# A window-attention start reordered: x alone on the queues, the fold around the group norm, tokens in 16 loads, norms spread two at a time

## The chip, the core and the metric

The kernel runs on one core of a Trainium2 chip. Its time is the device time of one execution in microseconds (us); lower is better. The core has a matrix engine (PE), a vector engine (DVE), an activation engine (ACT), GpSimd (POOL) and a synchronising engine (SP) that issues transfers. Each runs its own stream of instructions in order; they meet at semaphores. SP, ACT and POOL can issue DMA transfers, and all transfers share 16 DMA engines. PE writes to PSUM, from which the others copy ("evacuate") to SBUF.

## What is computed

The input is an image of 256 channels and 64 x 64 positions. Cut to what matters here:

```python
# layer 0: window attention over a group-normed image
xn = group_norm(x)                                # 32 groups of 8 channels
q, k = sigmoid(Wq xn), sigmoid(Wk xn)             # 8 heads of 32 channels
v = Wv xn, each head's vector scaled to length 1
for w in (1, 2, 4):                               # box of 64, 32, 16 positions a side
    attn = q . box_sum(k v^T)
    norm = q . box_sum(k)
    outs.append(attn / (norm + 1e-6))
x = x + Wout concat(outs) + bout
# layer 1: tokens of 256 values, causal attention with Wq, bq, Wk, bk, Wv, bv,
# a small feed-forward, then a mixture of two of eight experts
```

The causal layer's scores need only products of its weights, Wq^T Wk and its bias terms. The kernel works those out once, at its start ("the fold"), and parks them in DRAM until the causal layer.

## The kernel before, in words

`window_attention` loads the image `x` (4 MB) in four chunks of 1024 positions; each chunk comes in two transfers, channel half 0 on SP's queue and half 1 on ACT's. Then it issues, in the program's order, the six mask tables on ACT, the fold, the 32 token loads on SP (`t`, the image again with positions as rows) and `bo`, the output bias, on POOL. The group norm follows: `bn_stats` on DVE over half 0 and then half 1, a matmul with `groups` that averages over 8 channels (L264), four small DVE steps, a second such matmul (L272), a square root on ACT and a reciprocal on DVE. `norm` holds the means and scales with which DVE writes normalised chunks (L612).

`folded` (L743 to L800) transposes both weights on PE (L763), copies them with DVE (L764), multiplies them (L775, once per half `c`), forms the bias terms by matmuls of one column (L780, L785, L792), and writes four results to DRAM on SP (L798). It has a pool of its own.

`window_heads` runs twice, for head groups `hg` 0 and 1 (128 channels each). It projects each chunk to k and q (L519) and to v (L542), turns k (L575) and sums blocks (L586). What stands in the list `late` is run at chunk 0, behind its values. Then come two loops over "lists", each of which fills a 512-column PSUM bank for each of four heads. The first loop has 45 lists along columns of the image, the second 93 along eight strips `Y` of eight rows. `push` handles a list: mask matmuls (L353), score matmuls (L362, four heads on four groups of 32 rows), evacuation (L330 on ACT for five of eight, L332 on DVE), and, for the list before, the sums with v (L395, in `add`). PSUM has six rotating buffers for this, and two for the sums.

`norms` gives the steps for one strip's norms: `sum_up`, four `invert` steps, and three `spread_out` steps, each of which spreads one window's norm over the heads by a matmul (L479) and copies it (L482, ACT). `inner` (four or three DVE steps) prepares the inner part that `inside` feeds to PE (L414), `convolve` is the output projection (L507), `boxes` makes POOL work for the next strip. In the second loop `plan(at, tasks)` puts one task behind each list from number `at` on; `firsts[Y]` is a strip's first list.

PE and POOL follow the program's order in these loops, and in the list loops DVE and ACT too (`manual_schedule`). Elsewhere a scheduler orders each engine's work by when it expects it to be ready.

Of the kernel before, what the change touches and what calls it, by code (L numbers as in the profile page):

```python
# [19 lines left out]
P = 128  # L20
# [132 lines left out]
@with_exitstack  # L153
def conv_attn_hybrid(ctx: ExitStack, tc: tile.TileContext, a, out):
    nc = tc.nc

    const = ctx.enter_context(tc.tile_pool(name="const", bufs=1))
    ident = const.tile([P, P], F32, name="ident")
    make_identity(nc, ident)
    eps5 = const.tile([P, 1], F32, name="eps5")  # L160
    nc.vector.memset(eps5, 1e-5)

    tok = ctx.enter_context(tc.tile_pool(name="tok", bufs=1))
    t = tok.tile([P, NT, D], F32, name="t")

    dram = ctx.enter_context(tc.tile_pool(name="folded", bufs=1, space=bass.MemoryType.DRAM))
    low = ctx.enter_context(tc.tile_pool(name="low", bufs=1))
    iks = ctx.enter_context(tc.tile_pool(name="iks", bufs=1, reuse_waits="tile"))
    causal = Causal(tc, a, t, ident, eps5, low, iks)
    window_attention(tc, a, t, eps5, ident, causal, lambda psum: folded(tc, dram, psum, a, ident))  # L170
    big = ctx.enter_context(tc.tile_pool(name="l12big", bufs=1, reuse_waits="tile"))
    keep = ctx.enter_context(tc.tile_pool(name="l12keep", bufs=1, reuse_waits="tile"))
    given = Given(nc, a, keep, causal)
    x2 = causal_attention(tc, t, ident, eps5, causal, big, given)
    experts(tc, a, t, out, ident, eps5, given, x2)


def window_attention(tc, a, t, eps5, ident, causal, first):
# [5 lines left out]
    with ExitStack() as ctx:  # L184
# [23 lines left out]
        raws.append(load(3, vh.rearrange("p j e -> p (j e)")[:, 0:2048].rearrange("p (c n) -> p c n", c=DC)))  # L208
        tables = []
# [5 lines left out]
        causal.fold = first(psum)  # L215
        for i in range(NT):
            nc.sync.dma_start(out=t[:, i, :], in_=a["xT"][i * P : (i + 1) * P, :])
        bo = w.tile([P, D], F32, name="l0bo")
        nc.gpsimd.dma_start(out=bo, in_=a["L0_bout"].partition_broadcast(P))
# [30 lines left out]
        pt = psum()  # L250
        wide = sm.tile([P, 4, 32], F32, name="wide", bufs=1)
        nc.vector.tensor_copy(wide, sums.unsqueeze(1).to_broadcast([P, 4, 32]))
        nc.tensor.transpose(pt[:, 0:P], wide.rearrange("p w j -> p (w j)"), ident)
        nc.vector.tensor_copy(spreadh, pt[:, 0:P])


        mv = sm.tile([P, DC, 2], F32, name="mv")
        for c in range(DC):
            st = sm.tile([P, NQ, 6], F32, name="st")
            for j in range(NQ):  # L260
                nc.vector.bn_stats(out=st[:, j, :], in_=raws[j // 2][:, c, (j % 2) * 512 : (j % 2 + 1) * 512])
            nc.vector.bn_aggr(out=mv[:, c, :], in_=st)
        pm = psum()
        nc.tensor.matmul(pm[:, 0:DC], lhsT=groups, rhs=mv[:, :, 0], start=True, stop=True)  # L264
        gm = w.tile([P, DC], F32, name="gm")
        nc.vector.tensor_copy(gm, pm[:, 0:DC])
        d2 = sm.tile([P, DC], F32, name="d2")
        nc.vector.tensor_sub(d2, mv[:, :, 0], gm)
        nc.vector.tensor_mul(d2, d2, d2)
        nc.vector.tensor_add(d2, d2, mv[:, :, 1])  # L270
        pv = psum()
        nc.tensor.matmul(pv[:, 0:DC], lhsT=groups, rhs=d2, start=True, stop=True)  # L272
        rs = w.tile([P, DC], F32, name="rs")
        nc.scalar.activation(rs, pv[:, 0:DC], AF.Sqrt, bias=eps5)
        nc.vector.reciprocal(rs, rs)
        norm = [(gm[:, c : c + 1], rs[:, c : c + 1]) for c in range(DC)]

        late = []
# [19 lines left out]
def window_heads(tc, a, t, ident, hg, norm, raws, load, psum, pools, tables, consts, late, causal):  # L298
# [13 lines left out]
    nc.gpsimd.dma_start(out=wo, in_=a["L0_Wout"].rearrange("(w g p) e -> g p w e", g=2, p=P)[hg])  # L312
# [149 lines left out]
    def norms(boxed, rns):  # L462
# [14 lines left out]
        def spread_out(wi):  # L477
            pn = psum()
            nc.tensor.matmul(pn, lhsT=spreadh[32 * wi : 32 * wi + 32, :], rhs=r[32 * wi : 32 * wi + 32, :],  # L479
                             start=True, stop=True)  # L480
            rn = state["h"].tile([P, 512], F32, name=f"rn{wi}")
            nc.scalar.copy(rn, pn)  # L482
            rns.append(rn)

        return [sum_up] + [lambda j=j: invert(j) for j in range(4)], [lambda wi=wi: spread_out(wi) for wi in range(3)]
# [106 lines left out]
    with tc.manual_schedule(engines={mybir.EngineType.PE, mybir.EngineType.Pool}), ExitStack() as keys:  # L592
        with ExitStack() as vctx:
# [25 lines left out]
            for m in range(4):  # L619
                if m < 3:  # L620
                    normalise(m + 1)
                project(gs[m], m)
                values(gs[m], m)
                if m == 0:
                    while late:
                        late.pop(0)()
                if m:
                    block_sums(kp, m - 1)
                kp = turned(m)
# [14 lines left out]
            for m in range(4):  # L644
                for s in range(2):
                    for b in range(2):
# [4 lines left out]
                        )  # L651
            if hg == 0:
# [3 lines left out]

            steps, spreads = norms(boxed, strips[0]["rn"])
            for i, parts in enumerate(lists[1:]):
                push(parts)
                if i >= len(lists) - 9 and steps:  # L660
                    steps.pop(0)()
# [24 lines left out]
        for Y in range(8):  # L686
            at, after = firsts[Y], firsts[Y + 1]
            plan(at, lambda Y=Y: (outer(1, Y), outer(2, Y)))
            plan(at + 1, *(lambda wi=wi, Y=Y: strips[Y]["st"].append(inner(wi, Y)) for wi in (1, 2)))
            if Y == 0:  # L690
                plan(at + 1, *spreads)
            if Y < 7:
                plan(at, lambda Y=Y: ahead(Y + 1))
                end = plan(max(after - 5, at + 6), *(lambda n=n, Y=Y: got[Y + 1][0][n]() for n in range(5)))
                plan(max(end, after + 1), *(lambda n=n, Y=Y: got[Y + 1][1][n]() for n in range(3)))
# [47 lines left out]
def folded(tc, dram, psum, a, ident):  # L743
# [3 lines left out]
    with ExitStack() as tmp:  # L747
        s = tmp.enter_context(tc.tile_pool(name="foldsm", bufs=1, side="right"))
        mm = s.tile([P, DC, D], F32, name="mm")
        mb = s.tile([P, DC], F32, name="mb")  # L750
        wvu = s.tile([P, DC, D + 2], F32, name="wvu")
        nc.gpsimd.memset(wvu[:, :, 0:1], 0.0)
        bvc = s.tile([P, D + 2], F32, name="bvc")
        nc.gpsimd.memset(bvc[:, 0:1], 1.0)
        wT = {}
        for name in ("Wq", "Wk"):
            src = s.tile([P, DC, D], F32, name=f"f{name}")
            nc.scalar.dma_start(out=src, in_=a["L1_" + name].rearrange("(c p) e -> p c e", p=P))
            dst = s.tile([P, DC, D], F32, name=f"t{name}")
            for e in range(DC):  # L760
                pt = psum()[:, 0:D]
                for c in range(DC):
                    nc.tensor.transpose(pt[:, c * P : (c + 1) * P], src[:, c, e * P : (e + 1) * P], ident)  # L763
                nc.vector.tensor_copy(dst[:, e, :], pt)  # L764
            wT[name] = dst
        col = {}
        for name in ("bq", "bk"):
            col[name] = s.tile([P, DC], F32, name=f"f{name}")
            nc.scalar.dma_start(out=col[name], in_=a["L1_" + name].rearrange("(c p) -> p c", p=P))
        nc.scalar.dma_start(out=wvu[:, :, 1 : D + 1], in_=a["L1_Wv"].rearrange("(c p) e -> p c e", p=P))  # L770
        nc.scalar.dma_start(out=bvc[:, 1 : D + 1], in_=a["L1_bv"].partition_broadcast(P))
        for c in range(DC):
            pm = psum()[:, 0:D]
            for e in range(DC):
                nc.tensor.matmul(pm, lhsT=wT["Wq"][:, e, c * P : (c + 1) * P], rhs=wT["Wk"][:, e, :],  # L775
                                 start=(e == 0), stop=(e == DC - 1))
            nc.vector.tensor_copy(mm[:, c, :], pm)
            pb = psum()[:, 0:D]
            for e in range(DC):
                nc.tensor.matmul(pb[:, 0:1], lhsT=wT["Wk"][:, e, c * P : (c + 1) * P], rhs=col["bq"][:, e : e + 1],  # L780
                                 start=(e == 0), stop=(e == DC - 1))
            nc.vector.tensor_copy(mb[:, c : c + 1], pb[:, 0:1])
            pb = psum()[:, 0:D]
            for e in range(DC):
                nc.tensor.matmul(pb[:, 0:1], lhsT=wT["Wq"][:, e, c * P : (c + 1) * P], rhs=col["bk"][:, e : e + 1],  # L785
                                 start=(e == 0), stop=(e == DC - 1))
            nc.vector.tensor_copy(wvu[:, c, D + 1 :], pb[:, 0:1])
        bqs = s.tile([P, DC, P], F32, name="bqs")
        nc.vector.tensor_copy(bqs, col["bq"].unsqueeze(2).to_broadcast([P, DC, P]))
        pb = psum()[:, 0:D]  # L790
        for e in range(DC):
            nc.tensor.matmul(pb[:, 0:1], lhsT=bqs[:, e, :], rhs=col["bk"][:, e : e + 1],  # L792
                             start=(e == 0), stop=(e == DC - 1))
        nc.vector.tensor_copy(bvc[:, D + 1 :], pb[:, 0:1])
        out = []
        for src in (mm, mb, wvu, bvc):
            d = dram.tile(list(src.shape), F32, name=f"fold{len(out)}")
            nc.sync.dma_start(out=d, in_=src)  # L798
            out.append(d)
    return out  # L800
# [564 lines left out]
```

## Time and profile before

Three runs took 1961.94, 1963.89 and 1965.53 us; the median is 1963.89. The profiled execution took 1963.31 us with a span of 1961.6 us.

| stretch of the span (us) | what runs | PE busy | DVE | ACT | POOL | DMA share |
|---|---|---|---|---|---|---|
| 0 to 93 | loads, fold, group norm, projections of hg 0 | 63.31 | 50.80 | 28.44 | 21.71 | 0.56 |
| 93 to 198 | lists of columns, hg 0 | 102.56 | 48.04 | 64.14 | 74.32 | 0.14 |
| 198 to 503 | strips, hg 0 | 303.13 | 169.89 | 144.91 | 89.67 | 0.09 |
| 503 to 561 | projections of hg 1 | 55.59 | 38.55 | 26.37 | 15.70 | 0.40 |
| 561 to 664 | lists of columns, hg 1 | 100.70 | 45.51 | 62.19 | 55.10 | 0.14 |
| 664 to 998 | strips, hg 1 | 332.11 | 215.28 | 155.92 | 95.32 | 0.10 |
| 998 to 1961 | causal layer, experts | 910.3 | 445.4 | 298.3 | 86.9 | 0.02 |

Busy times are us in the stretch. A group's row in the profile names line, engine, operation, what it writes and reads (`ps<-r,spreadh`), shape and count. A waits row says who waited for whom: total us, how many times, the longest. The fp32 matmul of the program is two instructions ("passes") in the trace. Issues of transfers carry a q (ACTq, SPq) and are not counted as busy.

### The profile page before, as it was taken

The numbers are of one execution on the slowest core, as the hardware profiler recorded it, in microseconds if no ns is written. First come the engines' busy times: TensorE is split into PE (matmuls) and PEld (weight loads), VectorE is DVE, ScalarE is ACT, GpSimd is POOL, SyncE is SP. The second block draws the span as 40 slices with busy tenths as digits, with TensorE's granted clock in tenths as the row PEclk, the third lists the DMA queues.
The fourth block names the chain that finished last, engine by engine and source line by source line (L and its number), as shares of the span: only waits on it lengthen the run. The fifth ranks groups of instructions, "written<-read, shape, count | busy, mean of one in ns | idle before, by whom it ended". The sixth has DMA issues, their size and how long they took to land.

```text
span 1961.6 us, 50126 instructions
## 1 busy us (share of the span) xinstructions
PE 1867.7 (95%) x22286; PEld 1272.9 (65%) x22286; DVE 1013.5 (52%) x2154; ACT 780.3 (40%) x1295; POOL 438.8 (22%) x709
## 2 busy tenths in 40 slices
PE   3999999999999999999999999999999999789998
PEld 2666666666566667666665666665666666557777
DVE  4644555564654466666653435454554555543343
ACT  0566544444456645444413333233332333223322
POOL 1286233342255133432100000000000000031120
PEclk9999999999999999999999999999999999879999
DMA  8211100000331100002000000000000000010000
GB/s 246 75 56 41 40 14 14 19 19 13 112 88 37 49 19 19 13 13 51 13 2 1 0 1 0 1 1 1 0 1 0 1 1 1 1 43 22 22 22 22
DMA packets 66905, 53.58 MB, mean 27 GB/s; under 512 B 37568, under 2 KB 56792, under 8 KB 66688
## 3 DMA queue, kind: packets, MB, share of 16 engines
q1 hardware_dynamic: 57296, 31.87, 6.0%
q10 hardware_dynamic: 8128, 14.67, 2.1%
q0 software_dynamic: 1264, 3.84, 0.6%
q8 instruction: 174, 2.85, 0.6%
q14 instruction: 43, 0.35, 0.1%
HBM read 32.93 MB, written 17.44 MB: 26 GB/s over the span
## 4 chain that ended last, share of the span: by engine, by line
PE 43%; DVE 6%; ACT 3%; issue 1%; POOL 0%; ACTq 0%; DVEq 0%; POOLq 0%
PE po L1035 12%; PE pa L991 10%; PE ph L1299 6%; PE py L1319 6%; PE pt L1021 2%; PE pm L1092 1%; PE acc L395 1%; PE pm L1102 1%; PE ps L362 1%; PE ps L507 1%; DVE sT L1024 1%; DVE nbs L999 1%; DVE lnst L731 1%; PE pm L950 1%; ACT s L1004 1%
## 5 line engine op out<-in xcount | busy, mean ns | idle before, releaser
L330 ACT ACTIVATE pm<-ps 128x512 f32<-128x512 f32 (+24 forms) x690 | 358.4, 584 | 330.6 <-PE ps L362 176.8
L332 DVE TENSOR_SCALAR pm<-ps 128x512 f32<-128x512 f32 (+21 forms) x414 | 265.3, 668 | 265.2 <-PE ps L362 172.7
L362 PE MATMUL ps<-q,kh 32*128 32x217 f32 (+27 forms) x3872 | 213.1, 336 | 0.0
L395 PE MATMUL acc<-pm,vh 128*32 128x217 f32 (+27 forms) x3872 | 199.7, 329 | 0.0
L991 PE MATMUL pa<-k,qT 128*128 128x512 f32 (+3 forms) x416 | 180.2, 574 | 7.1 <-ACT qT L952 5.7
L362 PEld LDWEIGHTS ps<-q,kh 32*128 32x128 f32 x3872 | 161.2, 185 | 9.7
L1024 DVE COPY sT<-pt 128x512 f32<-128x512 f32 (+3 forms) x144 | 92.5, 642 | 143.1 <-PE pt L1021 142.9
L353 PE MATMUL ps<-table,table 32*128 32x184 bf16 (+36 forms) x2904 | 142.7, 245 | 5.4 <-issue 1.2
L395 PEld LDWEIGHTS acc<-pm,vh 128*32 128x32 f32 x3872 | 98.0, 109 | 71.7 <-issue 37.1
L430 POOL TENSOR_TENSOR y<-y,rn 128x512 f32<-128x512 f32 x32 | 40.9, 1277 | 432.8 <-DVE y L429 358.2
L993 ACT ACTIVATE s<-pa,v 128x512 f32<-128x512 f32 (+3 forms) x112 | 73.8, 661 | 152.2 <-PE pa L991 152.1
L991 PEld LDWEIGHTS pa<-k,qT 128*128 128x128 f32 x416 | 75.7, 191 | 89.3 <-issue 72.4
L353 PEld LDWEIGHTS <-table 32*128 32x128 bf16 x2904 | 57.0, 92 | 108.4 <-issue 97.6
L999 DVE TENSOR_REDUCE nbs<-s 128x1 f32<-128x512 f32 (+4 forms) x120 | 77.5, 651 | 80.6 <-ACT s L993 59.2
L1319 PE MATMUL py<-w,hT 128*128 128x256 f32 x512 | 111.8, 379 | 0.0
L1035 PE MATMUL po<-kh,sT 128*128 128x257 f32 x406 | 102.9, 395 | 8.7 <-DVE sT L1024 8.5
L1319 PEld LDWEIGHTS py<-w,hT 128*128 128x128 f32 x512 | 97.3, 190 | 15.7 <-issue 1.9
L362 PE MATMUL ps<-q,k 32*128 32x192 f32 (+30 forms) x1936 | 102.8, 337 | 0.0
L395 PE MATMUL acc<-pm,v 128*32 128x192 f32 (+30 forms) x1936 | 95.9, 326 | 0.6 <-issue 0.6
L507 PE MATMUL ps<-l0wo,y 128*128 128x256 f32 x384 | 90.7, 387 | 0.0
L1035 PEld LDWEIGHTS po<-kh,sT 128*128 128x128 f32 x406 | 74.7, 195 | 22.3 <-DVE sT L1024 12.7
L982 POOL MEMSET s<- 128x32 f32 x20 | 2.5, 124 | 376.5 <-PE pt L1021 348.4
(305 smaller groups left out, 2997.0 us busy)
## 6 DMA issues: line engine op xcount, KB each, us to landing
oscratch<-ov ACTq DMA_DIRECT2D x32, 256.0 KB
ov<-oscratch SPq DMA_DIRECT2D x32, 256.0 KB
t<-in_xT SPq DMA_DIRECT2D x32, 128.0 KB
vscratch<-v SPq DMA_DIRECT2D x32, 128.0 KB
vh<-vscratch SPq DMA_DIRECT2D x16, 256.0 KB
raw<-in_x ACTq DMA_DIRECT2D x7, 512.0 KB
raw<-in_x SPq DMA_DIRECT2D x7, 512.0 KB
out<-y SPq DMA_DIRECT2D x7, 512.0 KB
```

The source lines that it names most:

```text
L330: nc.scalar.activation(dst, src, AF.Relu)
L332: nc.vector.tensor_scalar_max(dst, src, 0.0)
L353: nc.tensor.matmul(got[h][:, spot].rearrange("p (y x) -> p y x", y=part.r1 - part.r0), lhsT=spread[hs, int(part.vertical), :], rhs=bias[hs ...
L362: nc.tensor.matmul(got[h][:, spot].rearrange("p (y x) -> p y x", y=part.r1 - part.r0), lhsT=keys[hs], rhs=q[hs, part.r0 : part.r1, part.c0 ...
L395: nc.tensor.matmul(out, lhsT=v, rhs=pm[:, h, spot].rearrange("p (y x) -> p y x", y=part.r1 - part.r0), start=fresh, stop=(left[key] == 0), ...
L507: nc.tensor.matmul(pt[:, i * D : (i + 1) * D], lhsT=ys[wi, Y][:, (2 * j + i) * P : (2 * j + i + 1) * P], rhs=wo[:, n, :], start=(n == 0), ...
L991: nc.tensor.matmul(pp[:, 0:m], lhsT=qTs[g][:, c, i * P - g * 512 : n - g * 512], rhs=x[b // 512][c][:, 0:m], start=(c == 0), stop=(c == DC ...
L999: nc.vector.tensor_reduce(nbs[:, at : at + 1], s[:, b : b + m], AX.X, ALU.max)
L1024: nc.vector.tensor_copy(sT[:, 0:full], pt[:, 0:full])
L1035: nc.tensor.matmul(acc, lhsT=sT[0:m, j * P : (j + 1) * P], rhs=rhs, start=(b == 0), stop=(m != P))
L1299: nc.tensor.matmul(ph, lhsT=w1v[:, e, c, f, :], rhs=x2[g][c], start=(c == 0), stop=(c == DC - 1))
L1319: nc.tensor.matmul(py, lhsT=hT[:, e, f, j * P : (j + 1) * P], rhs=w2v[:, e, f, :], start=(e + f == 0), stop=(e == 1 and f == FC - 1))
```

## The change

It touches the start of `window_attention`, `folded`, and three places in `window_heads`.

- `folded` becomes a generator in five pieces. It takes its room from `t`, which is loaded later, instead of a pool. Biases bq and bk become a 257th column of the turned weights, so one product gives the matrix and one bias term; the other bias matmuls share a PSUM bank. Its copies move from DVE to ACT.
- Its loads are issued directly behind x on ACT, and a square root on ACT follows; the six tables come after that.
- PE's order is written out: weight transposes, first group matmul, product of half 0, second group matmul, product of half 1. `rest` (the transpose for `spreadh`, the remaining fold, the load of `bo`) is put in `late`.
- The statistics run by arrival, chunk by chunk.
- `wo` is loaded behind chunk 0 instead of at the head of `window_heads`.
- The tokens come in 16 loads of 256 KB on ACT, one behind every second list of columns from list 1 on; POOL's additions of `bo` stand behind that loop.
- `spread_out` takes a pair of windows and then the third: two tasks instead of three; window 1's copy goes to DVE. `inner` is planned one list later.

```diff
@@ window_attention
+        folding = first(psum)
+        next(folding)
+        root = sm.tile([P, 1], F32, name="root", bufs=1)
+        nc.scalar.activation(root, eps5, AF.Sqrt)
         tables = []
...
-        causal.fold = first(psum)
-        for i in range(NT):
-            nc.sync.dma_start(out=t[:, i, :], in_=a["xT"][i * P : (i + 1) * P, :])
         bo = w.tile([P, D], F32, name="l0bo")
-        nc.gpsimd.dma_start(out=bo, in_=a["L0_bout"].partition_broadcast(P))
...
+        for j in range(NQ):
+            for c in range(DC):
+                nc.vector.bn_stats(out=st[:, c, j, :], in_=raws[j // 2][:, c, (j % 2) * 512 : (j % 2 + 1) * 512])
         for c in range(DC):
...
+            nc.vector.bn_aggr(out=mv[:, c, :], in_=st[:, c])
+        with tc.manual_schedule(engines={mybir.EngineType.PE}):
+            next(folding)
+            pm = psum()
+            nc.tensor.matmul(pm[:, 0:DC], lhsT=groups, rhs=mv[:, :, 0], start=True, stop=True)
+            next(folding)
...
+            pv = psum()
+            nc.tensor.matmul(pv[:, 0:DC], lhsT=groups, rhs=d2, start=True, stop=True)
+            rs = w.tile([P, DC], F32, name="rs")
+            nc.scalar.activation(rs, pv[:, 0:DC], AF.Sqrt, bias=eps5)
+            nc.vector.reciprocal(rs, rs)
+            next(folding)
+
+        def rest():
+            pt = psum()
+            nc.tensor.transpose(pt[:, 0:P], wide.rearrange("p w j -> p (w j)"), ident)
+            nc.scalar.copy(spreadh, pt[:, 0:P])
+            causal.fold = next(folding)
+            nc.gpsimd.dma_start(out=bo, in_=a["L0_bout"].partition_broadcast(P))
...
-        late = []
+        late = [rest]
@@ norms
-        def spread_out(wi):
-            pn = psum()
-            nc.tensor.matmul(pn, lhsT=spreadh[32 * wi : 32 * wi + 32, :], rhs=r[32 * wi : 32 * wi + 32, :],
-                             start=True, stop=True)
-            rn = state["h"].tile([P, 512], F32, name=f"rn{wi}")
-            nc.scalar.copy(rn, pn)
-            rns.append(rn)
+        def spread_out(wis):
+            pns = [psum() for _ in wis]
+            for wi, pn in zip(wis, pns):
+                nc.tensor.matmul(pn, lhsT=spreadh[32 * wi : 32 * wi + 32, :], rhs=r[32 * wi : 32 * wi + 32, :],
+                                 start=True, stop=True)
+            for wi, pn in zip(wis, pns):
+                rn = state["h"].tile([P, 512], F32, name=f"rn{wi}")
+                (nc.vector.tensor_copy if wi == 1 else nc.scalar.copy)(rn, pn)
+                rns.append(rn)
@@ window_heads
                 if m == 0:
                     while late:
                         late.pop(0)()
+                    nc.gpsimd.dma_start(out=wo, in_=a["L0_Wout"].rearrange("(w g p) e -> g p w e", g=2, p=P)[hg])
...
+            for i, parts in enumerate(lists[1:]):
+                push(parts)
+                if hg == 0 and i % 2 == 0 and i < NT:
+                    nc.scalar.dma_start(
+                        out=t[:, i : i + 2, :], in_=a["xT"][i * P : (i + 2) * P, :].rearrange("(j p) d -> p j d", p=P))
+                if i >= len(lists) - 9 and steps:
+                    steps.pop(0)()
...
-            plan(at + 1, *(lambda wi=wi, Y=Y: strips[Y]["st"].append(inner(wi, Y)) for wi in (1, 2)))
+            plan(at + 2, *(lambda wi=wi, Y=Y: strips[Y]["st"].append(inner(wi, Y)) for wi in (1, 2)))
@@ folded
+    for name in ("Wq", "Wk"):
+        nc.scalar.dma_start(out=src[name], in_=a["L1_" + name].rearrange("(c p) e -> p c e", p=P))
+    for name in ("q", "k"):
+        nc.scalar.dma_start(out=wT["W" + name][:, :, D], in_=a["L1_b" + name].rearrange("(c p) -> p c", p=P))
...
+    yield
+    for name in ("Wq", "Wk"):
         for e in range(DC):
...
+            nc.scalar.copy(wT[name][:, e, 0:D], pt)
+    yield
+    for c in range(DC):
+        pm = psum()
+        for e in range(DC):
+            nc.tensor.matmul(pm[:, 0 : D + 1], lhsT=wT["Wq"][:, e, c * P : (c + 1) * P], rhs=wT["Wk"][:, e, :],
                              start=(e == 0), stop=(e == DC - 1))
+        nc.scalar.copy(mm[:, c, :], pm[:, 0:D])
+        nc.scalar.copy(wvu[:, c, D + 1 :], pm[:, D : D + 1])
+        yield
```

## The prediction

> **What bounds the kernel now.** I read the page's slices first, then the waits of the first 60 us, then the start in order of time, and last the stretch around one spread of the norms. In the slices each character is a fortieth of the span (49 us) and each digit a busy share in tenths.
>
> ```profile
> PE   3999999999999999999999999999999999789998
> PEclk9999999999999999999999999999999999879999
> DMA  8211100000331100002000000000000000010000
> ```
>
> TensorE (PE) is full from the second slice to the end of the window stage, so two things can shorten that half: an earlier start, and less PE work in it. The first slice has PE at 3 and the DMA engines at 8.
>
> ```profile
> PE ps L763 <- DMA fWq<-in_L_Wq: 26.6, 1, 26.6
> SPq L217 <- DMA raw<-in_x: 11.5, 3, 4.6
> ```
>
> PE's first instruction waits 26.6 us for a weight that only the fold needs. The second row shows issues held back: eight x loads are out by 3.1 us, and the ninth issue of each queue waits for one of them to land.
>
> ```profile
> 6.17 14.97 ACTq L212 DMA_DIRECT2D table<-in_mask  x6
> 18.45 0.69 DVE L261 BATCH_NORM_STATS2 st<-vh 128x6 f32<-128x512 f32 x1 [2.20 <-DMA vh<-in_x]
> 23.76 0.37 DVE L262 BATCH_NORM_AGGREGATE mv<-st 128x2 f32<-128x48 f32 x1
> 26.59 1.08 PE L763 MATMUL ps<-ident,fWq 128*128 128x128 f32 x4 [26.59 <-DMA fWq<-in_L_Wq]
> 29.73 2.07 PE L775 MATMUL ps<-tWk,tWq 128*128 128x256 f32 x4
> 37.67 0.43 PE L264 MATMUL ps<-mv,groups 128*128 128x2 f32 x2
> 38.93 0.59 PE L272 MATMUL ps<-d,groups 128*128 128x2 f32 x2 [0.84 <-DVE d L270]
> 40.85 6.33 PE L519 MATMUL ps<-kh,l0Wk 128*128 128x512 f32 x8 [1.33 <-DVE kh L612]
> 47.01 3.60 PE L519 MATMUL ps<-kh,l0Wq 128*128 128x512 f32 x8
> ```
>
> Columns: start, length (us), engine, line, operation. The group norm's statistics are ready at 24.1, but its first matmul (L264) stands behind the whole fold in PE's order and runs at 37.67. The first projection (L519) starts at 40.85; from there PE hardly rests. So the path is: six tables, fold weights, fold, group norm, projection.
>
> **Start: x alone.** Last x packets land for L261 at 18.45. What shares the engines with them is in these stretches (last columns: DMA share, GB/s):
>
> ```profile
> 6.00:9.00 3.00, 0.00 (x0) 0.00 (x0) 1.87 (x3) 0.00 (x0) 1.85 (x6) 1.00 0.99 227
> 9.00:17.00 8.00, 0.00 (x0) 0.00 (x0) 3.17 (x5) 0.00 (x0) 0.00 (x0) 1.00 1.02 379
> ```
>
> From 6 to 9 the engines are full but move only 227 GB/s; in the DMA view of that stretch POOL's queue takes 44.7% of the engines' time for 0.10 of 0.68 MB. The first load in that queue is the broadcast of `bo`, which moves behind the first values. That gives back 3 us x (1 - 227/379) = 1.2 us; `wo`, moved too (0.39 MB at 379 GB/s), gives 1.0. The token loads go as well, but hardly overlap x. So x lands at about 18.45 - 2.2 = 16.2; a bound on either side: 15 and 17.5.
>
> Statistics: 16 BN_STATS of 0.61 us paced. Before, channel half 1 waited for half 0 (six were left at 20.1). Ordered by arrival only the last chunk's four remain: 16.2 + 2.4 + two aggregations 0.7 = 19.3, against 24.1.
>
> **Start: the fold.** The fold weights now stand right behind x in ACT's queue and the tables behind them. 256 KB at some 300 GB/s is 0.9 us, so Wq lands near 17, Wk near 18; the four-byte bias columns landed 0.2 us after Wk before, so I put them there again. PE order is transposes, L264's matmul, product c=0, L272's matmul, product c=1, projection. Eight transpose passes cost 1.1 us per weight (L763 row): over by 19.2. Four ACT copies follow (0.35 us for this size). Product c=0 costs 1.85 us paced, 2.07 by its row. If the copies come at once, c=0 runs 19.7 to 21.6 beside the group norm's small DVE steps (before: 1.26 us from L264 to L272). If ACT first finishes issuing the six tables, each waiting for a landing of x, Wq, Wk or a bias, the copies end near 21 and c=0 at 23. Then L272's matmul, and c=1 (1.9 us) covers the square root, reciprocal and first normalised blocks, which took 1.92 us before. Projection: 21.6 + 2.4 = 24.0, or 25.4. I take 24.5; bounds 22.5 and 27.5. Gain 40.85 - 24.5 = **16.3**. Next late are the fold's copies, no longer DMA.
>
> The rest of the fold (one transpose, 12 one-column passes) moves behind the first values, where PE is full, so nothing hides it: 13 passes at 0.11 us each (L542's pace once PE is fast) = 1.4; at the 0.21 of the cold stretch 2.8. Take **-1.5**. The removed copy work on DVE, the DRAM writes on SP and POOL's two later issues (0.7 and 0.8 us, on an engine idle there 4 us at a time) lie beside PE; without cover they would cost 1.5 us together.
>
> Here a rule of the Trainium skill is to be weighed. The rows say that eight 512-column passes took 6.33 us at 40.85 and 3.43 paced at 47.01, although PE had been at the fold since 29.7: the one-column passes did not speed the clock up. "TensorE: Matmul & The Clock Gate", Part 1, says some 3.4 us of sustained activity release the clock, and idle gaps throttle it again. By the rule, two products back to back with little between would warm PE before the projection: 2.7 us more gain. By the row, the projection starts cold again: none. I take the row, as gaps for the copies and the square root remain, and keep 2.7 for the range.
>
> **Tokens in 16 loads on ACT.** SP's 32 issues go; ACT gets 16, one behind every second list of columns (45 lists of about 2.4 us, so all are issued). Behind each on ACT stand the next list's evacuations, for which PE waits by way of six PSUM buffers. The nearest row is the store's issue in the same stage:
>
> ```profile
> 116.55 0.33 ACTq L407 DMA_DIRECT2D oscratch<-ov  x1
> 116.97 1.09 ACT L330 ACTIVATE pm<-ps 128x512 f32<-128x512 f32 x2 [0.46 <-PE ps L362]
> ```
>
> Even in this crowded list ACT idles 0.46 us, elsewhere over 1. An issue of 0.35 fits; where it doesn't, 16 x 0.35 = 5.6 us is the whole price. Below nothing it cannot go: PE is full there either way. Take **-0.5**. POOL's additions of `bo` (8 x 2.4 us) wait for the last load, issued at list 31; POOL was idle from 170.7 to 188.2, so they still end before the boxes are wanted.
>
> **Norms side by side.** L479 spreads one window's norm in two 32-row passes. Around it:
>
> ```profile
> 271.12 1.09 PE L395 MATMUL acc<-pm,vh 128*32 128x31 f32 x32
> 272.14 0.69 PE L479 MATMUL ps<-r,spreadh 32*128 32x512 f32 x1
> 272.68 0.59 PE L479 MATMUL ps<-r,spreadh 32*128 32x512 f32 x1
> 274.32 1.03 PE L395 MATMUL acc<-pm,vh 128*32 128x144 f32 x24
> 277.54 1.07 PE L395 MATMUL acc<-pm,vh 128*32 128x155 f32 x24
> 278.54 1.12 PE L479 MATMUL ps<-r,spreadh 32*128 32x512 f32 x2
> ```
>
> From L395 to L395 it is 3.20 and 3.22 us with a spread, 2.37 in the mean of 166 plain lists: 0.85 per spread, and 1.05 for the third, which stands alone before the convolution. The two paired matmuls use different 32 rows and different banks, as L362's four heads do: eight 512-column passes in 1.03 us at 493.8, where full-array passes take 0.43 each. So a pair costs what one did, and one of three goes: 16 strips x 0.9 = **14.4**. Bounds: 0, if they run in turn; 16.8 at 1.05. Against it speaks "TensorEngine Tiling", PSUM Bottleneck: row tiles speed PE but not the evacuation. The pair takes two of six buffers, and the next list then needs all four of the list before, evacuated some 1.9 us after its last matmul; PE reaches them after L395 and the pair, 1.9 us. By the rule up to 0.5 us is lost per strip, leaving 6.4; by the rows nothing. I take 14, as half of the heads run on other rows meanwhile. The second copy goes to DVE (0.67 us; DVE is 56% busy there). `inner` a list later is due soonest in the last strip, one list on; its four DVE steps (1.1 us) end about 0.4 us ahead of L414.
>
> **Sum.** 16.3 - 1.5 - 0.5 + 14 = 28.3. The profiled execution took 1963.31 (span 1961.6, 1.7 around it), 0.6 under the median of the runs: 1963.3 - 28.3 = **1935.0**.
>
> **Rivals.**
> - *The pairs bring nothing* (they run in turn, or wait for PSUM): 14.3 from the start alone, **1949**. For it: six buffers. Against: L362. Chance 0.13.
> - *The start gains less*: copies behind the tables, x no sooner, cold passes in the rest; projection at 27.5, rest 2.8: 10.5 + 13.5 = **1939**. Inside the range. Chance 0.2.
> - *It gains more*: projection at 22.5 and warm, pairs at 1.05: 18.4 + 2.7 - 1.5 + 16.8 = 36 : **1927**. Chance 0.1.
> - *Slower: the token issues block ACT.* The tables' six issues took 14.97 us, 2.5 each, waiting for landings. If each token issue waits likewise and PE with it, 0.5 us of slack off, 16 x 2.0 = 32 us eats the gain; it decides from 2.3 us per issue, and at 3.5 the time is **1983**. Against: the tables waited with the engines 95% to 100% busy, here 14%, and the store's issue takes 0.33. Chance 0.04.
> - Forecast: 0.53.
>
> **Range.** 1926 to 1947 holds the forecast, the smaller start, the larger gain and half of the first rival. A measurement of this kernel can tell 0.2% (3.9 us) from no change. Slower 0.04, the same 0.02 (between the rivals), faster 0.94.
>
> **What would show it.** PE's first projection at 24 to 25 us; L264's matmul near 19; the eight first passes again near 6.3 us; tokens' issues on ACT under 0.5 us; plain column lists still 2.4 us apart; spread slots 0.85 over a plain list, two per strip. It is wrong if the pair's slot is 1.7 over a plain list, or if waits of PE for ACT appear between the lists of columns.

## The result, and the profile after

The kernel after took 1930.45 us (median of four runs, 1929.66 to 1931.35), the kernel before beside it 1963.99. The ratio is 0.9836, with a 95% interval from 0.9824 to 0.9848: 33.5 us less, where 28.3 had been forecast (1935.0, range 1926 to 1947). The profiled execution took 1931.35 us, its span 1929.7.

The page's slices, 48 us each now:

```profile
PE   6999999999999999999989999999999999789998
PEclk9999999999999999999999999999999999889999
DMA  5332000001321100002000000000000000010000
```

PE stands at 6 in the first slice instead of 3. The DMA engines fell there from 8 to 5, and the tokens show as 3, 3, 2 in the slices behind. PE's one 8 in the middle covers 965 to 1013 us, where the causal layer begins: PE waits 4.15 us there for ACT, as it does in the kernel before (where the wait falls into another slice).

The start of PE in order of time (start, length, engine, line, operation):

```profile
15.89 1.97 PE L790 MATMUL ps<-ident,t 128*128 128x128 f32 x8 [15.89 <-DMA t<-in_L_Wq]
17.79 0.56 PE L265 MATMUL ps<-mv,groups 128*128 128x2 f32 x2
19.04 2.08 PE L796 MATMUL ps<-t 128*128 128x257 f32 x4 [0.69 <-ACT t L791]
20.91 0.43 PE L274 MATMUL ps<-d,groups 128*128 128x2 f32 x2
21.20 2.06 PE L796 MATMUL ps<-t 128*128 128x257 f32 x4
23.05 4.07 PE L531 MATMUL ps<-kh,l0Wk 128*128 128x512 f32 x8
26.95 3.60 PE L531 MATMUL ps<-kh,l0Wq 128*128 128x512 f32 x8
33.96 0.27 PE L282 MATMUL ps<-ident,wide 128*128 128x128 f32 x1
34.07 0.95 PE L805 MATMUL ps<-t 128*128 128x1 f32 x8
34.88 0.58 PE L808 MATMUL ps<-t 128*128 128x1 f32 x4
```

The group norm's first matmul runs at 17.79 (before 37.67), the first projection at 23.05 (40.85). The first eight projection passes take 4.07 us, where they took 6.33: the clock is full about 1 us after the projection's start. The last three rows are what `rest` put behind the values.

A comparison of the two traces by stage, from PE's starts at the matmuls that open each stage (for the strips the scores of their second list):

| stage | before (us) | after (us) | difference |
|---|---|---|---|
| to the first projection | 40.85 | 23.05 | -17.80 |
| first projection to first score matmul | 53.57 | 52.72 | -0.85 |
| lists of columns, hg 0 | 111.90 | 114.76 | +2.86 |
| strips, hg 0 | 298.19 | 289.28 | -8.91 |
| projections of hg 1 | 56.49 | 60.50 | +4.01 |
| lists of columns, hg 1 | 112.56 | 112.64 | +0.08 |
| strips, hg 1 | 298.30 | 288.57 | -9.73 |
| the rest, to the end of the span | 989.76 | 988.14 | -1.62 |
| span | 1961.6 | 1929.7 | -31.9 |

So the gain came from the start and from the strips, and two stages gave some back. The experiments take these rows one at a time.

### The profile page after: what moved, and what is told of

The parts are those of the page before. It is cut to its first block, busy times and chain, and to the rows that moved or that the text cites. A ratio compares the mean times of both kernels' runs of the same rounds, so it can differ in the third digit from the quotient of the medians.

```text
span 1929.7 us, 50077 instructions
## 1 busy us (share of the span) xinstructions
PE 1846.7 (96%) x22278; PEld 1265.7 (66%) x22278; DVE 1019.0 (53%) x2160; ACT 774.0 (40%) x1289; POOL 439.8 (23%) x709
## 4 chain that ended last, share of the span: by engine, by line
PE 44%; DVE 6%; ACT 3%; issue 1%; POOL 0%; ACTq 0%; POOLq 0%; DVEq 0%
PE po L1052 12%; PE pa L1008 10%; PE ph L1316 6%; PE py L1336 6%; PE pt L1038 2%; PE pm L1109 2%; PE acc L405 1%; PE ps L372 1%; PE pm L1119 1%; PE ps L519 1%; DVE sT L1041 1%; DVE nbs L1016 1%; DVE lnst L747 1%; PE pm L967 1%; ACT s L1021 1%
## 5 line engine op out<-in xcount | busy, mean ns | idle before, releaser
L405 PE MATMUL acc<-pm,vh 128*32 128x217 f32 (+27 forms) x3872 | 199.7, 329 | 0.0
L363 PE MATMUL ps<-table,table 32*128 32x184 bf16 (+37 forms) x2904 | 141.0, 245 | 5.0 <-ACT pm L340 2.0
L405 PEld LDWEIGHTS acc<-pm,vh 128*32 128x32 f32 x3872 | 98.0, 109 | 71.8 <-issue 37.1
L405 PE MATMUL acc<-pm,v 128*32 128x192 f32 (+30 forms) x1936 | 96.1, 326 | 0.5 <-issue 0.5
L519 PE MATMUL ps<-l0wo,y 128*128 128x256 f32 x384 | 90.7, 387 | 0.0
```

The source lines that it names most:

```text
L363: nc.tensor.matmul(got[h][:, spot].rearrange("p (y x) -> p y x", y=part.r1 - part.r0), lhsT=spread[hs, int(part.vertical), :], rhs=bias[hs ...
L405: nc.tensor.matmul(out, lhsT=v, rhs=pm[:, h, spot].rearrange("p (y x) -> p y x", y=part.r1 - part.r0), start=fresh, stop=(left[key] == 0), ...
L519: nc.tensor.matmul(pt[:, i * D : (i + 1) * D], lhsT=ys[wi, Y][:, (2 * j + i) * P : (2 * j + i + 1) * P], rhs=wo[:, n, :], start=(n == 0), ...
```

## Experiments

### The pairs, alone and left out

```diff
# e1_pairs_alone: the kernel before, with
-        def spread_out(wi):
+        def spread_out(wis):
...
-            plan(at + 1, *(lambda wi=wi, Y=Y: strips[Y]["st"].append(inner(wi, Y)) for wi in (1, 2)))
+            plan(at + 2, *(lambda wi=wi, Y=Y: strips[Y]["st"].append(inner(wi, Y)) for wi in (1, 2)))
# e2_no_pairs: the kernel after, with the same lines the other way round
```

> The kernel before with only the pairs of norms (spread_out by pairs, inner one list later). Theory: each strip loses the slot of one spread, read as 1.0 us per strip between the two traces, so 16 x 1.0 = 16 us less: 1948, with the start unchanged (first projection at 40.85). Rival 'the pairs gave little and the start gave most': 1958 or more. Rival 'the gain comes from moving inner, not from pairing': the first spread's slot would grow by 0.8 us over its length before.

> The kernel after with the norms spread one by one again. Theory: 16 us more than after, 1946.5; the start stays at 23.05. If the two parts only add up, before minus e1 equals e2 minus after within 2 us; if one hides the other, they differ.

e1 took 1943.42 us beside 1962.27 (ratio 0.9894, 0.9873 to 0.9914), e2 1946.23 (0.9909, 0.9888 to 0.9930). In e1 the strips take 289.67 and 289.20 us, 17.6 less than before; its first projection is at 41.06. In e2 they are back at 298.26 and 297.50, and the projection is at 22.98. Before minus e1 is 18.9 us, and e2 minus after, which did not run side by side, 15.8. That is 3.1 us apart, more than the 2 us that the expectation allowed, but the intervals of the two ratios leave room for it. The traces are closer: the pairs take 17.6 us from the strips in e1 and 17.9 between e2 and after. So the parts add up, some 18 for the pairs and 16 for the rest.

Where it comes from shows in the kernel after, around one strip's spreads (L490 is the spread, L405 the sums with v, L519 the convolution):

```profile
252.71 1.09 PE L405 MATMUL acc<-pm,vh 128*32 128x31 f32 x32
253.73 0.70 PE L490 MATMUL ps<-r,spreadh 32*128 32x512 f32 x2
253.94 0.55 PE L363 MATMUL ps<-table,table 32*128 32x155 bf16 x4
254.26 0.59 PE L490 MATMUL ps<-r,spreadh 32*128 32x512 f32 x2
255.91 1.03 PE L405 MATMUL acc<-pm,vh 128*32 128x144 f32 x24
256.87 0.69 PE L490 MATMUL ps<-r,spreadh 32*128 32x512 f32 x1
259.12 1.08 PE L405 MATMUL acc<-pm,vh 128*32 128x155 f32 x24
260.13 2.21 PE L519 MATMUL ps<-l0wo,y 128*128 128x256 f32 x9
```

From L405 to L405 it is 3.20 us with two spreads side by side, the same 3.20 that one spread took before. The two first passes start together at 253.73, the two second ones at 254.26. The next list's mask matmuls on the two free groups of rows start 0.2 us behind them. The second slot (255.91 to 259.12) is as long as before, and the convolution now follows L405 directly: the spread that stood alone there, 1.05 us, is gone. Moving `inner` cost nothing: no wait for it shows, and the first slot did not grow by the 0.8 us that e1's second rival asked for.

### All three at once

```diff
-        return ..., [lambda: spread_out((0, 1)), lambda: spread_out((2,))]
+        return ..., [lambda: spread_out((0, 1, 2))]
```

> The kernel after with all three windows' norms spread in one task. If only the rows of the array count, one more slot goes in each strip: 16 x 0.85 = 13 us less than after, 1917. If PSUM's six buffers limit it (three taken by the norms, and the next list needs four), the next list waits for the copies of the norms, about 0.8 us in each strip: 1930 or a little more, with waits of PE on ACT or DVE copies behind the spreads.

It took 1929.54 us (ratio 0.9825, 0.9806 to 0.9844), no better than the kernel after; the strips take 289.53 and 288.86 us. The waits of PE in e3's strips, and one of these waits in order of time (the list behind the spreads):

```profile
PE ps L363 <- ACT rn L494: 4.2, 7, 0.6
```

```profile
253.42 1.09 PE L405 MATMUL acc<-pm,vh 128*32 128x31 f32 x32
256.23 0.38 PE L363 MATMUL ps<-table,table 32*128 32x155 bf16 x9 [0.59 <-ACT rn L494]
257.44 1.03 PE L405 MATMUL acc<-pm,vh 128*32 128x144 f32 x24
```

PE waits for a copy of the norms, some 0.6 us in each of seven strips of head group 0; in the strips of the kernel after there is no such wait. The list that carries all three takes 4.02 us from L405 to L405 and the next one 2.53, together 6.55; with pairs the same two take 3.20 and 3.21, together 6.41. Without its wait the slot of three would take 3.43 us, 1.06 over a plain list's 2.37, where one or two spreads take 0.83. The wait is for the copy that frees a PSUM buffer, so by this releaser it is the six buffers more than the array that decide against the third; a run with more buffers wasn't made.

### The start: which part of it

Four kernels undo or isolate one part each.

```diff
# e11_tokens_alone: the kernel before, with the token loads moved
-        for i in range(NT):
-            nc.sync.dma_start(out=t[:, i, :], in_=a["xT"][i * P : (i + 1) * P, :])
...
+                if hg == 0 and i % 2 == 0 and i < NT:
+                    nc.scalar.dma_start(
+                        out=t[:, i : i + 2, :], in_=a["xT"][i * P : (i + 2) * P, :].rearrange("(j p) d -> p j d", p=P))
# e5_fold_first: the kernel after, with all of the fold ahead of the first group matmul
             next(folding)
+            next(folding)
+            next(folding)
+            causal.fold = next(folding)
             pm = psum()
# e6_stats_by_half: the kernel after, with
+        for c in range(DC):
             for j in range(NQ):
-            for c in range(DC):
# e7_bo_wo_first: the kernel after, with the loads of bo and wo at their old places
```

> The kernel before with only the token loads moved (16 on ACT among the lists of columns, POOL's additions behind them). The fold still precedes the group norm, the tables still precede the fold's weights. Theory that the order of the fold made the start: the weights land some 3 us sooner because nothing shares the engines with them, the first projection moves from 40.85 to about 37, and 2 to 3 us are lost again among the first lists of columns: 1962. Rival that the loads made it: first projection near 30, time 1952.

> The kernel after with the whole fold ahead of the group norm in PE's order. Theory: products, 12 one-column passes and their copies stand before the first group matmul; 2 x 1.9 + 12 x 0.21 = 6.4 us, from about 19 us, then 5.3 us to the first projection as before (2.4 + 1.92 and small steps): near 30 us instead of 23.05, less 1.4 us that no longer stand behind the first values: 1936. If the place of the fold hardly matters and only the loads do: first projection under 25, 1931.

> The kernel after with the statistics in the order half 0, then half 1. Theory: DVE had time left while x arrived and the scheduler still mixes the halves; x's last landing sets the end, so less than 1.5 us later: first projection between 23 and 24.5, 1930 to 1932. Rival: eight statistics of half 1 stand behind the last landing, 2.4 us later: 1933.

> The kernel after with the loads of bo and wo at their old places at the start. Theory: the broadcast of bo slows all engines for 3 us as before (227 GB/s instead of 392 between 6 and 9 us) and wo's 0.39 MB takes 1 us: x lands 2.2 us later, the group norm's first matmul at 20.0 instead of 17.79, first projection near 25. Rival: x's landing doesn't bind, since the fold's copies end at 19.3; then less than 0.7 us later.

| kernel | time (us) | ratio to before, interval | first group matmul | first projection |
|---|---|---|---|---|
| before | 1963.99 | 1 | 37.67 | 40.85 |
| e11_tokens_alone | 1964.53 | 1.0009 (0.9999 to 1.0019) | 32.85 | 36.02 |
| e5_fold_first | 1936.20 | 0.9858 (0.9835 to 0.9881) | 25.06 | 28.48 |
| e7_bo_wo_first | 1932.92 | 0.9846 (0.9828 to 0.9865) | 21.36 | 26.40 |
| e6_stats_by_half | 1932.23 | 0.9844 (0.9822 to 0.9865) | 20.48 | 24.89 |
| after | 1930.45 | 0.9836 (0.9824 to 0.9848) | 17.79 | 23.05 |

In the times alone e5, e6, e7 and the kernel after can't be told apart, since their intervals overlap; what follows rests on the traces.

The loads without the rest of the change bring 4.8 us to the first projection (e11), and none to the time: the same token issues lengthen its lists of columns from 111.9 to 114.9 us, and PE's clock falls to half at the turn of the head groups, which it had not in the profile before. There the fold still stood first:

```profile
22.05 1.09 PE L764 MATMUL ps<-ident,fWq 128*128 128x128 f32 x4 [22.05 <-DMA fWq<-in_L_Wq]
36.02 5.67 PE L517 MATMUL ps<-kh,l0Wk 128*128 128x512 f32 x8 [1.32 <-DVE kh L610]
```

Its weights land at 22.05, 6 us later than in the kernel after, because the six tables precede them, and 14 us pass from there to the projection; in the kernel after it is 7.2. In e5 the place of the fold alone costs 5.4 us:

```profile
22.64 1.70 PE L805 MATMUL ps<-t 128*128 128x1 f32 x8
24.21 0.99 PE L808 MATMUL ps<-t 128*128 128x1 f32 x4
25.06 0.57 PE L268 MATMUL ps<-mv,groups 128*128 128x2 f32 x2
28.48 5.47 PE L531 MATMUL ps<-kh,l0Wk 128*128 128x512 f32 x8 [1.37 <-issue]
```

The twelve one-column passes take 2.4 us here on the cold clock, where behind the values they take 1.3. The eight first projection passes are slow again, 5.47 us.

e6 went past its limit: 1.5 us had been put, and the projection moved by 1.84. DVE in e6:

```profile
16.19 2.45 DVE L259 BATCH_NORM_STATS2 st<-raw 128x6 f32<-128x512 f32 x4
18.56 1.27 DVE L259 BATCH_NORM_STATS2 st<-vh 128x6 f32<-128x512 f32 x2
```

Six statistics stand behind the last of half 0, not eight and not four. In the kernel after, the last statistics end at 17.1. The first group matmul thus comes 2.7 us later, but a part is hidden: the first product, which stands behind it, waited for the fold's copies anyway.

e7 shows what the broadcast of `bo` and the load of `wo` do together. The stretch from 6 to 9 us in e7 and then in the kernel after (last columns: DMA share, GB/s), and the last statistics in e7:

```profile
6.00:9.00 3.00, 0.00 (x0) 0.00 (x0) 2.15 (x4) 0.00 (x0) 1.85 (x6) 1.00 0.94 208
```

```profile
6.00:9.00 3.00, 0.00 (x0) 0.00 (x0) 2.46 (x5) 0.00 (x0) 0.14 (x1) 1.00 1.03 392
```

```profile
18.23 2.47 DVE L260 BATCH_NORM_STATS2 st<-vh 128x6 f32<-128x512 f32 x4 [1.03 <-DMA vh<-in_x]
```

With `bo` and `wo` in front, busy engines move about half as much. The last statistics wait for x until 18.23, where in the kernel after they ran without a wait at 14.67: at least 3.6 us, not the 2.2 that had been counted. The fold's weights stand behind x and shift with it (the transposes start at 19.22 instead of 15.89), and the projection comes 3.35 us later. Which share is the broadcast's and which `wo`'s, no run separates.

### The tables in front of the fold's copies

```diff
# e8_tables_late: the kernel after, with the table loads moved from behind `root` into `rest`
         def rest():
...
+            for i, s in enumerate(tables):
+                nc.scalar.dma_start(out=s, in_=a[f"mask{i}"])
             causal.fold = next(folding)
```

> The kernel after with the six tables issued behind the fold's copies on ACT. Theory: in after the four copies stood behind the last table issue until 18.06 and the first product ran at 19.04; without the tables they run from about 16.5, the product by 18.2 beside the group norm's small steps, and the first projection comes at 22.1 instead of 23.05: 0.9 us less. If another wait ends there (the bias column, the group norm itself), nothing moves.

ACT in the kernel after, which shows the cause:

```profile
15.40 2.62 ACTq L216 DMA_DIRECT2D table<-in_mask  x5
18.06 1.20 ACT L791 COPY t<-ps 128x256 f32<-128x256 f32 x4 [2.80 <-DMA table<-in_mask]
```

In e8 the copies start at 16.65, and the projection comes at 22.43, 0.62 us sooner than in the kernel after and 0.32 sooner than in its second execution. The first product now follows the group matmul at once (18.44), and the second group matmul waits for that product's four passes alone. In the time nothing shows: 1930.33 us, against 1929.49 for the kernel after beside it.

### The tokens on SP

```diff
-                    nc.scalar.dma_start(
+                    nc.sync.dma_start(
                         out=t[:, i : i + 2, :], ...
```

> The kernel after with the 16 token loads issued from SP at the same places. Theory: ACT's issue of the third load stood 1.66 us and held the evacuations behind it, so PE lost 1.3 us in one list and up to 2.9 us over the lists of columns of head group 0; from SP that goes and the stage from the first mask to the end of list 44 is 2 to 3 us shorter: 1928. Rival: the lists are slower because the transfers themselves disturb something else; then nothing changes.

It took 1934.29 us (0.9856, 0.9838 to 0.9875), slower than expected. The lists of columns took 112.18 us instead of 114.76, as expected, but that does not decide against the rival: SP's work isn't in written order there, the scheduler drew the tokens to the start, and all sixteen were issued by 48.7 us, before the lists. SP and ACT in e4:

```profile
5.71 22.85 SPq L670 DMA_DIRECT2D t<-in_xT  x10
```

```profile
20.51 3.22 ACTq L216 DMA_DIRECT2D table<-in_mask  x4
23.78 1.20 ACT L791 COPY t<-ps 128x256 f32<-128x256 f32 x4 [3.76 <-DMA t<-in_xT]
```

Ten token loads compete with the fold's weights and hold the tables' issues, these hold the copies on ACT, and the projection comes at 28.58. So this run became a test of "x alone": tokens at the start cost 5.5 us even with the new order of the fold.

What the tokens do on ACT, in the kernel after (ACT, then PE):

```profile
93.24 0.33 ACTq L417 DMA_DIRECT2D oscratch<-ov  x1
93.69 1.66 ACTq L670 DMA_DIRECT2D t<-in_xT  x1
95.45 1.08 ACT L340 ACTIVATE pm<-ps 128x512 f32<-128x512 f32 x2 [2.24 <-POOL ik L655]
```

```profile
96.10 0.39 PE L363 MATMUL ps<-table,table 32*128 32x64 bf16 x6 [1.31 <-ACT pm L340]
```

Thirteen of the 16 issues take 0.37 to 0.47 us. The third stood for 1.66 us, evacuations waited behind it, and PE lost 1.31 us; the sixth and the fourteenth stood for 1.10 and 0.92 and cost nothing. List by list against e4, from one sum with v (L405) to the next, the third load's list is 1.50 us longer. Four more are 0.2 to 0.5 longer, and in these the load is issued directly behind a store, so that the two hold ACT for some 0.8 us. But for the first, all other lists agree within 0.1 us, loads or not, so it is the issues and not the transfers that disturb. What the third load waits for wasn't settled. The releaser says POOL, but POOL ends an addition every 0.4 us there, and the issue ended 0.36 us behind such an end here and 0.24, 0.39 and 0.12 in e12, e8 and e2. In e11, where the fold does not lie in `t`, the third load stands for 1.51 us too.

### Both together, with SP in written order

```diff
# e10_all: e8 and e9 (below) together, tokens on nc.sync, and for head group 0
-            keys.enter_context(tc.manual_schedule(engines={mybir.EngineType.DVE, mybir.EngineType.Activation}))
+            keys.enter_context(tc.manual_schedule(engines={..., mybir.EngineType.SP}))
```

> The kernel after with both of these edits, and the token loads on SP in the written order behind the loads of vh. Theory: 0.9 from the tables, 2.6 from ACT's lists of columns (112.2 instead of 114.8 us), 3 to 4 from the turn of the head groups: 1924 (1922 to 1927). If the token loads disturb the lists from SP too, the column stage stays at 114.8.

It took 1936.20 us (0.9849, 0.9834 to 0.9864), 6.7 more than the kernel after beside it. The start is kept (projection at 22.54), but the lists of columns take 121.93 us. ACT in e10:

```profile
84.98 0.59 ACT L416 COPY ov<-acc 128x512 f32<-128x512 f32 x1
93.53 0.34 ACTq L417 DMA_DIRECT2D oscratch<-ov  x1
93.97 1.57 ACT L340 ACTIVATE pm<-ps 128x512 f32<-128x512 f32 x3 [8.40 <-DMA t<-in_xT]
```

On SP all 16 token loads went out one behind the other from 84.35. The store's issue on ACT stood until 93.53 behind the landing of such a load, with the evacuations behind it; PE waited 7.4 us, and its clock was half for 10.2 us from 89.2. The trace's semaphores show why: the transfers of SP and ACT take turns on eight landing semaphores, and the store was given that of the token load issued at 88.01, whose last packet landed at 93.46. This is the slower rival of the prediction in one place: an issue on ACT that waits for another transfer holds PE. Spread among the lists, the tokens avoid it. No version tried beats the kernel after by more than its runs differ.

### The clock at the turn of the head groups

The projections of hg 1 took 4 us more than before. PE in the kernel after:

```profile
479.81 1.10 PE L531 MATMUL ps<-kh,l0Wk 128*128 128x512 f32 x2 [2.13 <-issue]
482.69 5.49 PE L531 MATMUL ps<-kh,l0Wk 128*128 128x512 f32 x6 [1.79 <-DVE kh L624]
487.97 3.71 PE L531 MATMUL ps<-kh,l0Wq 128*128 128x512 f32 x8
```

PE waits twice for x's first chunk, 2.13 and 1.79 us (before 2.15 and 0.49), and the passes between are slow: the granted clock was half from 481.4 for 6.8 us. Two runs asked whether the wait causes it.

```diff
# e9_second_x_on_sp: the kernel after, with
-                raw = raws[m] if raws else load(m)
+                raw = raws[m] if raws else load(m, second=nc.sync)
```

> The kernel after with both channel halves of x loaded on SP for head group 1. Theory: PE's clock falls to half at the turn of the head groups because PE waits 3.9 us in two pieces for the first chunk, whose half 1 is issued last and shares the engines with the second chunk; with the first chunk whole at the head of one queue the wait is near 2.5 us, the clock stays full, and the stretch from that projection to the first mask takes 56 to 57 us instead of 60.5. Rival: the half clock there is the phase of its own window, in which case it comes or not as in the other runs (56.5 to 60.8).

> The kernel after unchanged, a second execution with a profile. If the half clock at the turn of the head groups belongs to the program, it is there again for 6.8 us; if it is the phase of a window that the program doesn't set, it may be missing or 3.4 us, with the stretch from 56.5 to 60.8 us.

e9 took 1928.91 us (0.9818, 0.9805 to 0.9831), e12 1929.49 (0.9821, 0.9807 to 0.9834): the same. In e9 the second wait shrank (2.52 and 0.77), and the half clock was there for 3.4 us; the stretch took 58.46. In e12 the waits were 2.27 and 0.64 and the half clock lasted 6.8 us (59.63). So a shorter wait alone doesn't do it.

What decides can be read from where the clock changes. In the kernel after, half clock begins at 481.38, 1010.44, 1198.17 and 1655.56 us; the distances are 155, 55 and 134 times 3.413 us. In all fourteen profiles every change of the clock lies on such a grid, each with its own start. Call the time from one point of the grid to the next a clock window. Here are three clock windows of the kernel after, and then one of e6, which kept its clock (columns: busy time of PE, weight loads, DVE, ACT and POOL, granted clock, DMA share, GB/s):

```profile
477.96:481.38 3.42, 1.10 (x2) 0.30 (x2) 1.33 (x3) 0.23 (x1) 1.30 (x1) 1.00 0.85 281
481.38:484.79 3.41, 2.10 (x3) 1.07 (x4) 2.75 (x9) 0.00 (x0) 0.00 (x0) 0.50 0.37 150
484.79:488.20 3.41, 3.41 (x5) 1.35 (x5) 1.95 (x7) 0.60 (x1) 0.00 (x0) 0.50 0.00 0
```

```profile
477.54:480.95 3.41, 1.51 (x12) 0.39 (x7) 1.07 (x3) 1.93 (x3) 0.00 (x0) 1.00 0.92 286
```

PE's busy share of such clock windows, over all fourteen profiles of this study:

| profile | PE's waits at the turn (us) | lowest share in one clock window | share in the first at half clock | half clock there (us) | projections of hg 1 (us) |
|---|---|---|---|---|---|
| before | 2.15 + 0.49 | 0.58 | | none | 56.49 |
| e6 | 2.26 + 0.71 | 0.44 | | none | 56.71 |
| e4 | 2.21 + 0.19 | 0.37 | 0.93 | 3.4 | 57.67 |
| e3, e2, e9 | 2.21 to 2.52 + 0.77 to 1.46 | 0.32 to 0.41 | 0.93 to 1.00 | 3.4 | 58.46 to 59.16 |
| e12, e10 | 2.27 + 0.64, 2.74 + 0.78 | 0.31 to 0.34 | 0.77 to 0.81 | 6.8 | 59.63, 59.75 |
| e5, e1, after, e8, e7, e11 | 2.10 to 2.42 + 1.07 to 1.93 | 0.29 to 0.32 | 0.62 to 0.81 | 6.8 | 59.85 to 60.77 |

At this place the clock halves behind a clock window in which PE was busy for at most 0.41, and not at 0.44 or more. It stays half for a second one where PE was busy for 0.81 or less of the first. (Elsewhere in the traces single ones with up to 0.63 were followed by half clock, so these shares belong to this place.) The shortest wait of all, e4's, fell into one clock window and halved the clock; a longer one, e6's, was divided between two and did not. That is the rival: a window whose phase the program doesn't set, as "TensorE: Matmul & The Clock Gate" in the Trainium skill, Part 1, describes (a free-running one of 3.4 us). The page has an idle window slow the clock; here one that was busy for up to 0.41 of its length was enough. The profile before escaped, so the 4 us need not be a difference of the two kernels; e1 and e11, nearest to the kernel before, have the half clock too. An estimate from its trace: laid over its waits at a hundred other starts, the grid has a clock window at 0.41 or less in 59.

## Why the prediction was right, point by point

| term | predicted (us) | measured (us) | by |
|---|---|---|---|
| first projection sooner | -16.3 (to 24.5) | -17.8 (to 23.05) | trace after |
| clock sooner full | 0 (bound -2.7) | -2.3 | 6.33 to 4.07 us for eight passes |
| rest of the fold behind the values | +1.5 | +1.4 | 33.96 to 35.33 |
| tokens on ACT | +0.5 (bound 5.6) | +2.9; 2.6 against e4 | lists of columns |
| pairs | -14 (bound -16.8) | -17.6 (e1), -18.6 (after) | strips |
| turn of the head groups | not there | +4.0 | clock, in this execution |
| rest of the span | not there | -1.6 | not traced; half clock there for 44 us instead of 50 |

- *The start* was right in its path and nearly in size. x landed sooner than put: the last statistics began at 14.67, not 16.2. `bo` and `wo` together held x back by 3.6 us or more (e7), where 2.2 had been counted. The copies did stand behind the tables' issues and ended at 19.3, which cost 0.3 to 0.6 us (e8). One reading was wrong without harm: with four loads of x on each queue, the issue held back is a queue's fifth, the ninth of both together.
- *The clock* was the step that failed. The page's rule had been weighed against the row, and the row was taken, because gaps for the copies and the square root were to remain. In the kernel after they were too short: PE was busy for the whole clock window from 20.58 to 23.99, with the products and the first projection pass. From there the passes start 0.43 us apart instead of 0.86. In its second execution such a window ended at 22.2, before the projection. In the kernel before, the clock window from 32.5 to 35.9 was just as full and freed nothing, and so was that from 21.9 to 25.3 in e5; one-column passes made up part of the first and most of the second. So the row was true, but of a sequence with one-column passes between the products and the projection, and these did not bring the clock up.
- *The tokens* were undersized. The price of an issue was right (0.37 us). Two things were missed: that an issue may stand, which one did at PE's cost, and that a load directly behind a store uses up the 0.46 us that ACT had left there. Of the prediction's own signs of being wrong, one came, waits of PE for ACT between the lists of columns:

```profile
PE ps L363 <- ACT pm L340: 1.7, 3, 1.3
```

- *The pairs* were undersized too. What was allowed for PSUM, 0.4 us of the total, was not needed: two windows ran side by side without a wait, and only three hit the evacuation (e3). The removed slot is the one that stood alone before the convolution, 1.05 us and not 0.9. That makes 16.8; the other 0.8 to 1.8 us are not explained.
- *The slower rival* didn't happen in the kernel after, but its mechanism did in e10, for one issue of 8 us.

That the gain is within 5.2 us of the forecast is partly luck: the misses on the start, the clock and the pairs (7.4 to 8.4 us more gain) stand against 6.4 us lost at the tokens and the turn. The rival "It gains more" (1927, chance 0.1) had those three nearer than the forecast did.

## What to carry to other kernels

A path at the start is shortened by its order more than by its loads: moving the token loads alone gave 4.8 us and no time, the order with the tokens still at the start 12.3 (e4), both together 17.8. Matmuls on separate groups of rows run side by side until the buffers for their results run out, so count the buffers before pairing or tripling. An issue of a transfer placed on a busy engine costs little by itself; ask what it can wait for, because everything behind it on that engine waits too. And a wait of the matrix engine costs more than its length where it leaves one clock window mostly idle.

## What the runs showed of the hardware

- One broadcast load of 128 KB in POOL's queue, with 384 KB of `wo` behind it, nearly halved what the busy DMA engines moved for 3 us (208 against 392 GB/s).
- The granted clock changes on a grid of 3.41 us whose start differs from execution to execution. At the turn it fell to half at waits of 2.4 us in sum (e4) and stayed full at waits of 3.0 (e6); half clock lasted 3.4 or 6.8 us there, and the stage was up to 4.3 us longer.
- A clock window that PE filled mostly with one-column passes did not bring the clock up (21.9 to 25.3 us in e5), one of 257- and 512-column passes did (20.6 to 24.0 us in the kernel after).
- Two spreads side by side took the same 3.20 us slot as one.
